# Token shift and turn of the gated part's features: from TensorE transposes to DRAM round trips and VectorE block transposes, in the middle blocks

## The chip, the cores and the metric

The kernel runs on one core of a Trainium2 chip. The metric is the device time of one execution in microseconds. The median of three runs of the kernel before is 3990.55 us (3989.72 to 3990.79). The profile is of one further execution with a time of its own.

## The reference

The input x is 8 sequences of 512 tokens with 256 features, fp32. A "macaron" of three parts runs over it: half of a local block, a global attention, half of a second local block (the same weights).

```python
x = x + 0.5 * ffn(layernorm(x));  x = x + attn(layernorm(x));  x = x + 0.5 * ffn(layernorm(x))

def layer(x):                                 # ffn: two layers of this, DEPTH = 2
    h = shift_token(x)                        # features 128..255 come from the token before (0 for token 0)
    q, k, v = split(h @ wqkv)                 # 8 heads of 64; l2norm, rotary, window of 128
    x = x + local_attention(q, k, v) @ wo
    h = shift_token(x)
    h = (h - mean(h)) / sqrt(var(h) + 1e-5) * lg + lb
    a, g = split(h @ w1 + b1)                 # the gated part, 682 hidden features
    return x + (a * gelu(g)) @ w2 + b2
```

The global attention has 16 heads of 16 features over all 512 tokens, each with its own 256x256 slice of the output weight. The change concerns the gated part from `h = shift_token(x)` to the input of `h @ w1`.

## The kernel before, in words

A sequence lies in SBUF as four tiles of 128 tokens (partitions) by 256 features, y[:, t, :]. Matrix products need the features on the partitions, so activations are turned again and again.

Three streams of work are recorded: streams 0 and 1 (`stream`), which each take four sequences through their first and second local block (eight blocks, n = 0 to 7, of two layers: `attention`, then `glu`), and the global stream (`global_heads`), which takes the sequences one by one through the 16 global heads between their two local blocks. All three are Python generators, pulled in turn; a `yield` ends a chunk. Nothing is issued at that time: `Plan.record` notes each operation with its rank (the order of recording) and its dependencies. `Plan.order` then writes out a fixed order for each engine: it runs through time with a cost for each operation (`Plan.cost`) and gives an engine, of the operations that can start within 40 ns of the first, the one of lowest rank. A tile is given a buffer of its tag's ring when its first user is placed. A DMA costs the plan 2000 ns, its bytes at 170 per ns behind the DMAs before it, and 300 ns; all of a DRAM tile counts as one region. `Plan.issue` emits the instructions in that order, so each engine and SP's queue work strictly in it, and on the chip semaphores hold each back until its data is there. Since one line issues everything, all rows of the profile bear L369 and are told apart by their tiles.

`FAR` marks the blocks whose attention turns by way of DRAM: n = 1 to 6. There the normed q and k are transposed by VectorE in blocks of 32 by 32 and `turned_far` writes the tile to DRAM and reads it back in four DMAs, one for each 32 partitions, so that the blocks come to their places; the attention weights go the same way (`turned_quarters`). In blocks 0 and 7, TensorE transposes against the identity (`transposed`).

The gated part (`glu`) has one form for all blocks. `shifted` turns the second half of the features with four TensorE transposes (operands const_ident, ypool_y), and VectorE copies the result out of PSUM one column to the right (zpool_z); column 0 is zeroed by GpSimd. Four more transposes turn it back (const_ident, zpool_z), and the PSUM bank `sh` holds the shifted half by tokens. VectorE takes statistics of both halves (`layernorm_stats`; GpSimd computes the power -1/2) and norms eight pieces of 128x128 into two tiles of tag qn (`normalize`). After the chunk's end, eight transposes turn these (const_ident, work_qn) into two PSUM banks, and VectorE scales them into hT, two tiles of tag z. Then come the products with w1 (zpool_z, wpool_w), gelu on ScalarE, the gate on VectorE, and the products with w2.

Tags have few buffers: z, qn and p have two for each stream, `both` two in all, and there are eight PSUM banks. All DMAs of the middle go through SP's queue.

Of the kernel before, what the change touches and what calls it, by code (L numbers as in the profile page):

```python
# [9 lines left out]
F32 = mybir.dt.float32  # L10
AF = mybir.ActivationFunctionType
ALU = mybir.AluOpType
# [3 lines left out]
P = 128  # L16
B, N, D = 8, 512, 256
NT = N // P
# [12 lines left out]
FAR = True  # L31
# [344 lines left out]
def macaron(ctx: ExitStack, tc: tile.TileContext, x, weight, wqkv, wo, w1, w2, b2, vecs, qk_scales, rotary, out):  # L376
    nc = plan = Plan()
# [4 lines left out]
    const, xpool, wpool, ypool, zpool, work = (pool(name) for name in ("const", "xpool", "wpool", "ypool", "zpool", "work"))  # L382
# [4 lines left out]
    xs = {}  # L387
# [40 lines left out]
    tabs, vec = [], []  # L428
# [46 lines left out]
    def layernorm_stats(halves, small=small):  # L475

        mv = small.tile([P, NT, 2], F32, tag="mv")
        for t, pieces in enumerate(halves):
            st = small.tile([P, len(pieces), 6], F32, tag="bnst", width=12)
            for i, piece in enumerate(pieces):  # L480
                nc.vector.bn_stats(st[:, i, :], piece)
            nc.vector.bn_aggr(mv[:, t, :], st.rearrange("p a b -> p (a b)"))
        ve = small.tile([P, NT], F32, tag="ve")
        nc.vector.tensor_scalar_add(ve, mv[:, :, 1], 1e-5)
        rstd = small.tile([P, NT], F32, tag="rstd")
        nc.gpsimd.tensor_tensor(rstd, ve, nhalf[:, :NT], ALU.pow)
        return mv, rstd

    def normalize(dst, src, mv, rstd, t):
        nc.vector.tensor_scalar(dst, src, mv[:, t, 0:1], rstd[:, t : t + 1], ALU.subtract, ALU.mult)  # L490
# [8 lines left out]
    def bank(shape):  # L499
        return psum.tile(shape, F32, tag="bank", width=N)  # L500

    def transposed(src, c):

        pt = bank([P, NT, P])
        for t in range(NT):
            nc.tensor.transpose(pt[:, t, :], src(t, c), ident)
        return pt.rearrange("p t q -> p (t q)")

    def shifted(src, k):

        z = zpool.tile([P, N + 1], F32, tag=f"z{k}", bufs=2)
        nc.gpsimd.memset(z[:, 0:1], 0.0)
        nc.vector.tensor_copy(z[:, 1:], transposed(src, 1))
        return z

    def turned_far(tile_):


        _, n, _, m, _ = tile_.shape
        flat = tile_.rearrange("p j b h c -> p (j b h c)")  # L520
        d = dram.tile([P, n, 4, m * 32], F32, tag="turned", bufs=8, width=2 * N)
        nc.sync.dma_start(out=d.rearrange("p j b m -> p (j b m)"), in_=flat)
        for b in range(4):
            rows = tile_[32 * b : 32 * b + 32].rearrange("q j a h c -> q j a (h c)")
            nc.sync.dma_start(out=rows, in_=d[:, :, b].rearrange("(a q) j m -> q j a m", a=4))
# [25 lines left out]
            rows = tile_[32 * b : 32 * b + 32].rearrange("q j a h c -> q j a (h c)")  # L551
            nc.sync.dma_start(out=rows, in_=d[:, :, :, b].rearrange("a q j m -> q j a m"))

    quarters_of = {}

    def attention(k, y, l, far):
        wqkv_sb, wo_sb = attention_weights[l]
# [248 lines left out]
            yield  # L806
        project(NT - 1, o)

    def glu(k, y, step, xb):
        l = step % DEPTH  # L810
        w1_sb, ends_sb, w2_sb = glu_weights[step]

        z = shifted(lambda t, c: y[:, t, c * P : (c + 1) * P], k)
        sh = bank([P, NT, P])
        for t in range(NT):
            nc.tensor.transpose(sh[:, t, :], z[:, t * P : (t + 1) * P], ident)
        hn = [work.tile([P, NT, P], F32, tag=f"qn{k}", bufs=2) for _ in range(2)]
        mv, rstd = layernorm_stats([[y[:, t, :P], sh[:, t, :]] for t in range(NT)])
        for t in range(NT):
            normalize(hn[0][:, t, :], y[:, t, :P], mv, rstd, t)  # L820
            normalize(hn[1][:, t, :], sh[:, t, :], mv, rstd, t)
        yield
        hT = []
        for c in range(2):
            h = zpool.tile([P, N + 1], F32, tag=f"z{k}", bufs=2)
            nc.vector.tensor_scalar(
                h[:, :N], transposed(lambda t, c: hn[c][:, t, :], c), vec[l][:, c : c + 1], vec[l][:, 2 + c : 3 + c], ALU.mult, ALU.add
            )
            hT.append(h)
        bias = vec[l][:, 4:].rearrange("p (s m) -> p s m", s=2)  # L830
        us = []
        for m in range(FULL):
            if m < 4:
                if m % 2 == 0:
                    pair = work.tile([P, 2, N], F32, tag=f"p{k}", bufs=2)
                u = pair[:, m % 2]
            else:
                u = work.tile([P, N], F32, tag=f"qn{k}", bufs=2)
            us.append(u)
            ag = {}  # L840
            for s in (1, 0):
                ag[s] = bank([P, N])
                with plan.together():
                    for c in range(2):
                        nc.tensor.matmul(
                            ag[s], lhsT=w1_sb[:, c, s, m * P : (m + 1) * P], rhs=hT[c][:, :N], start=(c == 0), stop=(c == 1)
                        )
            nc.scalar.activation(u, ag[1], AF.Gelu, bias=bias[:, 1, m : m + 1])
            nc.vector.scalar_tensor_tensor(u, ag[0], bias[:, 0, m : m + 1], u, ALU.add, ALU.mult)
            if m % 2 == 1:  # L850
                yield

        u = work.tile([P, N], F32, tag=f"qn{k}", bufs=2)
        us.append(u)
        nc.gpsimd.memset(u, 1.0)
        ag = bank([P, 2, N // 2])
        with plan.together():
            for turn in range(2):
                half = slice(turn * N // 2, (turn + 1) * N // 2)
                for c in range(2):  # L860
                    nc.tensor.matmul(
                        ag[: TAIL + LAST, turn],
                        lhsT=ends_sb[:, c, TAIL * turn : TAIL * turn + TAIL + LAST],
                        rhs=hT[c][:, half],
                        start=(c == 0),
                        stop=(c == 1),
                    )
        for turn in range(2):
            half = slice(turn * N // 2, (turn + 1) * N // 2)
            a_ = slice(TAIL * turn, TAIL * turn + LAST)  # L870
            g_ = slice(TAIL * (1 - turn), TAIL * (1 - turn) + LAST)
            nc.scalar.activation(u[a_, half], ag[g_, turn], AF.Gelu, bias=bias[g_, 1, FULL : FULL + 1])
            nc.vector.scalar_tensor_tensor(
                u[a_, half], ag[a_, turn], bias[a_, 0, FULL : FULL + 1], u[a_, half], ALU.add, ALU.mult
            )
        yield
        pys = {}
        for t in (0, 2, 1, 3):
            py = bank([P, D])
            pys[t] = py  # L880
            with plan.together():
                for m in range(FULL):
                    nc.tensor.matmul(py, lhsT=us[m][:, t * P : (t + 1) * P], rhs=w2_sb[:, m, :], start=(m == 0), stop=False)
            if t < 2:
                continue
            with plan.together():
                for at, q in ((0, t - 2), (TAIL, t)):
                    rows = slice(at, at + LAST + 1)
                    nc.tensor.matmul(
                        pys[q],  # L890
                        lhsT=us[FULL][rows, q * P : (q + 1) * P],
                        rhs=w2_sb[rows, FULL, :],
                        start=False,
                        stop=True,
                    )
            for q in (t - 2, t):
                nc.vector.tensor_add(y[:, q, :], pys[q], y[:, q, :])
                if l == DEPTH - 1:
                    nc.vector.scalar_tensor_tensor(xb[:, q, :], y[:, q, :], 0.5, xb[:, q, :], ALU.mult, ALU.add)
            yield  # L900

    def stream(k, blocks):

        for n, (b, second) in enumerate(blocks):
            while second and (b, True) not in done:
                next(others, None)
            y = layernorm(xs[b], k)
            yield
            for l in range(DEPTH):
                step = DEPTH * n + l  # L910
                yield from attention(k, y, l, FAR and 0 < n < len(blocks) - 1)
                yield from glu(k, y, step, xs[b])

                if k == 1 and step + 1 < DEPTH * len(blocks):
                    glu_weights.append(load_glu((step + 1) % DEPTH))
                if l == 0 and n + 1 < len(blocks) and blocks[n + 1][0] not in xs:
                    load_x(blocks[n + 1][0])
            done.add((b, False))
            if second:
                nc.sync.dma_start(out=out[b].rearrange("(t p) c -> p t c", p=P), in_=xs[b])  # L920
# [194 lines left out]
```

## Time and profile before

| what | value |
|---|---|
| median of three runs | 3990.55 us |
| the profiled execution's own time | 3989.82 us |
| its span | 3988.0 us |
| TensorE matmul, busy | 3924.2 us (98%), 24192 instructions |
| VectorE, busy | 2419.2 us (61%), 6832 |
| ScalarE, busy | 1780.9 us (45%), 4560 |
| GpSimd, busy | 1217.0 us (31%), 1154 |
| DMA, SP's queue | 357.00 MB, 381120 packets, 30.4% of 16 engines |
| granted TensorE clock, mean | 0.997 |

Engines: PE is TensorE's matmul, PEld its weight load (which lies beside matmuls), DVE is VectorE, ACT ScalarE, POOL GpSimd, SP SyncE, which only issues DMAs. Groups of instructions are shown as: line, engine, operation, what it writes <- what it reads, shapes, count | busy us in the union of its times, mean ns of one | idle time of the engine ahead of it and what ended that. Timelines are shown as start and length in us, then the merged instructions. A transpose on TensorE stands there as a matmul with const_ident. Ends of matmuls are modelled, so a busy TensorE is not one at its peak.

### The profile page before, as it was taken

The page shows a single profiled execution, that of the slowest core. Times are in us where ns is not written, and L with a number is a line of the kernel's source. Part 1 is how long each engine was busy: PE and PEld are TensorE (multiplying, and loading weights), DVE is VectorE, ACT ScalarE, POOL GpSimd, SP SyncE. Part 2 cuts the span into 40 slices and gives each one's busy share as a digit, 9 for nine tenths or more (in the row PEclk, how much of TensorE's full clock was granted, in tenths as well). Part 3 has the DMA queues.
Part 4 walks back from the last instruction along what each step waited for, and adds up shares of the span by engine and source line. Part 5 has one row for each costly group of instructions (what it writes and reads, how often), then busy time and mean ns, then how long its engine had stood idle before and what let it go on. Part 6 is the DMA issues. An engine that isn't in the chain of part 4 may idle for free.

```text
span 3988.0 us, 68204 instructions
## 1 busy us (share of the span) xinstructions
PE 3924.2 (98%) x24192; PEld 2714.1 (68%) x24192; DVE 2419.2 (61%) x6832; ACT 1780.9 (45%) x4560; POOL 1217.0 (31%) x1154
## 2 busy tenths in 40 slices
PE   8999999999999999999999999999999999999998
PEld 5565776767767667676666767767777667687665
DVE  7585655756556675665756657566547565535673
ACT  5564433534334454453444445344435343314562
POOL 6242413424224242332423324242214232103240
PEclk9999999999999999999999999999999999999999
DMA  3001533524335243352433524334225243210000
GB/s 115 3 21 35 151 92 110 150 82 119 92 117 147 76 123 100 103 150 73 145 96 108 149 73 127 93 120 132 82 70 149 72 126 95 65 32 9 1 23 11
DMA packets 382325, 362.69 MB, mean 91 GB/s; under 512 B 50880, under 2 KB 326944, under 8 KB 381984
## 3 DMA queue, kind: packets, MB, share of 16 engines
q1 hardware_dynamic: 381120, 357.00, 30.4%
q8 instruction: 192, 3.15, 0.3%
q10 hardware_dynamic: 864, 1.33, 0.1%
q14 instruction: 149, 1.22, 0.1%
HBM read 216.61 MB, written 124.78 MB: 86 GB/s over the span
## 4 chain that ended last, share of the span: by engine, by line
PE 83%; DVE 5%; ACT 2%; POOL 1%; issue 1%; DMA 0%; SPq 0%; DVEq 0%; ACTq 0%; POOLq 0%
PE psum_bank L369 83%; ACT work_p L369 2%; DVE work_qn L369 1%; DVE work_p L369 1%; DVE small_ss L369 0%; POOL small_rn L369 0%; DVE small_bnst L369 0%; DVE xpool_x L369 0%; POOL small_rstd L369 0%; DVE ypool_y L369 0%; DVE small_mv L369 0%; ACT work_qn L369 0%; POOL work_t L369 0%; ACT work_sq L369 0%; DVE work_both L369 0%
## 5 line engine op out<-in xcount | busy, mean ns | idle before, releaser
L369 PE MATMUL psum_bank<-work_xw,work_e 128*128 128x256 f32 x4096 | 957.1, 383 | 2.5 <-ACT work_e L369 1.4
L369 PEld LDWEIGHTS psum_bank<-work_xw,work_e 128*128 128x128 f32 x4096 | 760.5, 190 | 182.4 <-issue 39.2
L369 ACT ACTIVATE work_p<-work_p,small_nmax,small_rn 128x192 f32<-128x192 f32 (+2 forms) x1024 | 543.3, 532 | 369.9 <-DVE small_nmax L369 269.1
L369 PE MATMUL psum_bank<-wpool_wqkv,zpool_z 128*128 128x512 f32 x1536 | 702.6, 597 | 0.4 <-ACT zpool_z L369 0.3
L369 POOL TENSOR_TENSOR work_t<-work_qn,const_tab 128x256 f32<-128x256 f32 x512 | 382.7, 768 | 789.9 <-ACT work_qn L369 774.0
L369 PE MATMUL psum_bank<-zpool_z,wpool_w 128*128 128x512 f32 x1280 | 558.9, 595 | 1.3 <-DVE zpool_z L369 1.2
L369 POOL TENSOR_TENSOR work_p<-work_p,small_ri 128x768 f32<-128x768 f32 (+1 forms) x192 | 270.1, 1408 | 946.9 <-DVE small_ri L369 501.2
L369 POOL TENSOR_TENSOR small_rn<-small_ss,const_nhalf 128x8 f32<-128x8 f32 x256 | 480.5, 1878 | 107.3 <-DVE small_ss L369 100.9
L369 PE MATMUL psum_bank<-work_wa,work_gz 128*128 128x256 f32 x2048 | 479.7, 381 | 3.4 <-DVE work_gz L369 3.4
L369 PEld LDWEIGHTS psum_bank<-wpool_wqkv,zpool_z 128*128 128x128 f32 x1536 | 284.2, 191 | 279.4 <-issue 262.7
L369 ACT ACTIVATE work_e<-psum_bank 128x512 f32<-128x512 f32 x512 | 298.5, 596 | 356.2 <-PE psum_bank L369 355.9
L369 DVE SCALAR_TENSOR_TENSOR xpool_x<-psum_bank,gsmall_rinv,xpool_x 128x256 f32<-128x256 f32 x512 | 242.6, 475 | 335.6 <-PE psum_bank L369 332.3
L369 PEld LDWEIGHTS psum_bank<-zpool_z,wpool_w 128*128 128x128 f32 x1280 | 242.8, 191 | 296.8 <-issue 272.1
L369 PEld LDWEIGHTS psum_bank<-work_wa,work_gz 128*128 128x128 f32 x2048 | 383.0, 190 | 70.2 <-issue 11.0
L369 ACT COPY work_qn<-psum_bank 128x512 f32<-128x512 f32 x256 | 148.4, 582 | 422.7 <-PE psum_bank L369 351.0
L369 DVE TENSOR_REDUCE small_ss<-work_sq 128x8 f32<-128x512 f32 x256 | 173.4, 678 | 184.0 <-ACT work_sq L369 182.9
L369 PE MATMUL psum_bank<-wpool_wo,work_o 128*128 128x256 f32 x1024 | 245.8, 383 | 1.1 <-ACT work_o L369 0.7
L369 DVE SCALAR_TENSOR_TENSOR work_p<-psum_bank,const_vec,work_p 128x512 f32<-128x512 f32 x128 | 95.8, 749 | 243.6 <-PE psum_bank L369 146.4
L369 PE MATMUL psum_bank<-wpool_w,work_p 128*128 128x256 f32 x1024 | 243.1, 380 | 0.4 <-ACT work_e L369 0.4
L369 DVE COPY work_xw<-psum_bank 128x512 f32<-128x512 f32 x256 | 173.9, 680 | 114.0 <-PE psum_bank L369 112.6
L369 DVE CUSTOM_DVE_ANT_0 work_p<-psum_bank,const_near_mask 128x192 f32<-128x192 f32 x576 | 172.3, 352 | 93.6 <-PE psum_bank L369 91.4
L369 PEld LDWEIGHTS psum_bank<-wpool_wo,work_o 128*128 128x128 f32 x1024 | 190.2, 190 | 48.4 <-issue 16.1
(86 smaller groups left out, 4941.4 us busy)
## 6 DMA issues: line engine op xcount, KB each, us to landing
work_p<-dram_quarters SPq DMA_DIRECT2D x576, 128.0 KB
dram_quarters<-work_p SPq DMA_DIRECT2D x288, 192.0 KB
dram_turned<-work_both SPq DMA_DIRECT2D x96, 512.0 KB
work_both<-dram_turned SPq DMA_DIRECT2D x384, 128.0 KB
work_wa<-in_weight_dram SPq DMA_DIRECT2D x128, 256.0 KB
wpool_w<-in_w_dram SPq DMA_DIRECT2D x48, 640.0 KB
work_hT<-work_gz SPq DMA_DIRECT2D x512, 32.0 KB
dram_turned<-work_p SPq DMA_DIRECT2D x48, 256.0 KB
```

Source lines behind the costliest of these rows:

```text
L369: getattr(getattr(nc, op.engine), name)(*map(real, args), **{k: real(a) for k, a in kw.items()})
```

## The change

In the blocks n = 1 to 6 (`far`) the gated part gets its shifted half by way of DRAM: a DRAM tile for each stream, made once by `later`, holds 513 rows of 128 features with a row of zeros at its head. The second half of y is written to it from row 1 on, in two DMAs (tiles 0 to 2, then tile 3), and rows 0 to 511 are read back into an SBUF tile `sh` of tag qn. The normed features are written in an order by blocks of 32 columns into one tile of tag p; VectorE transposes this tile in place in blocks of 32 by 32, and `turned_far` places the blocks by one write to DRAM and four reads. hT is then scaled out of SBUF. Blocks 0 and 7 keep the form of before.

```diff
+    def later(k):
+        if k not in later_of:
+            zeros = work.tile([1, P], F32, tag="t2", bufs=2, width=N)
+            nc.gpsimd.memset(zeros, 0.0)
+            d = dram.tile([P, N + 1], F32, tag=f"later{k}")
+            nc.sync.dma_start(out=d[0:1, :P], in_=zeros)
+            later_of[k] = d.rearrange("p w -> (p w)").rearrange("(n f) -> n f", f=P)
+        return later_of[k]
...
-    def glu(k, y, step, xb):
+    def glu(k, y, step, xb, far):
...
-        z = shifted(lambda t, c: y[:, t, c * P : (c + 1) * P], k)
-        sh = bank([P, NT, P])
+        if far:
+            sh = work.tile([P, NT, P], F32, tag=f"qn{k}", bufs=2)
+            tokens = later(k)
+            for tiles in (slice(0, NT - 1), slice(NT - 1, NT)):
+                rows = tokens[1 + tiles.start * P : 1 + tiles.stop * P, :]
+                nc.sync.dma_start(out=rows.rearrange("(t p) f -> p t f", p=P), in_=y[:, tiles, P:])
+            nc.sync.dma_start(out=sh, in_=tokens[:N, :].rearrange("(t p) f -> p t f", p=P))
+        else:
+            z = shifted(lambda t, c: y[:, t, c * P : (c + 1) * P], k)
+            sh = bank([P, NT, P])
+            for t in range(NT):
+                nc.tensor.transpose(sh[:, t, :], z[:, t * P : (t + 1) * P], ident)
+        mv, rstd = layernorm_stats([[y[:, t, :P], sh[:, t, :]] for t in range(NT)])
+
+        if far:
+            hn = work.tile([P, 2, 4, NT, P // 4], F32, tag=f"p{k}", bufs=2, width=2 * N)
+            part = lambda c, t: hn[:, c, :, t, :]
+            split = lambda u: u.rearrange("p (b c) -> p b c", c=P // 4)
+        else:
+            hn = work.tile([P, 2, NT, P], F32, tag=f"p{k}", bufs=2, width=2 * N)
...
+            normalize(part(0, t), split(y[:, t, :P]), mv, rstd, t)
+            normalize(part(1, t), split(sh[:, t, :]), mv, rstd, t)
+        if far:
+            flat = hn.rearrange("p j b t c -> p (j b t c)")
+            nc.vector.transpose(flat, flat)
+            turned_far(hn)
         yield
...
+            if far:
+                to, back = to.rearrange("p (t a q) -> p t a q", t=NT, a=4), hn[:, c].rearrange("p a t q -> p t a q")
+            else:
+                back = transposed(lambda t, c: part(c, t), c)
+            nc.vector.tensor_scalar(to, back, vec[l][:, c : c + 1], vec[l][:, 2 + c : 3 + c], ALU.mult, ALU.add)
```

More of the change, by code (lines that the diff above doesn't have):

```diff
@@ L552, in turned_quarters @@
             nc.sync.dma_start(out=rows, in_=d[:, :, :, b].rearrange("a q j m -> q j a m"))
-    quarters_of = {}
+    quarters_of, later_of = {}, {}
+    def later(k):
[6 more added lines that the diff above has]
+        return later_of[k]
     def attention(k, y, l, far):
@@ L807, in attention @@
         project(NT - 1, o)
-    def glu(k, y, step, xb):
+    def glu(k, y, step, xb, far):
         l = step % DEPTH
         w1_sb, ends_sb, w2_sb = glu_weights[step]
-        z = shifted(lambda t, c: y[:, t, c * P : (c + 1) * P], k)
-        sh = bank([P, NT, P])
-        for t in range(NT):
[L816 to L821, printed above, removed]
+        if far:
[17 more added lines that the diff above has]
+            hn = work.tile([P, 2, NT, P], F32, tag=f"p{k}", bufs=2, width=2 * N)
+            part = lambda c, t: hn[:, c, t, :]
+            split = lambda u: u
+        for t in range(NT):
+            normalize(part(0, t), split(y[:, t, :P]), mv, rstd, t)
[4 more added lines that the diff above has]
+            turned_far(hn)
         yield
@@ L825, in glu @@
             h = zpool.tile([P, N + 1], F32, tag=f"z{k}", bufs=2)
-            nc.vector.tensor_scalar(
-                h[:, :N], transposed(lambda t, c: hn[c][:, t, :], c), vec[l][:, c : c + 1], vec[l][:, 2 + c : 3 + c], ALU.mult, ALU.add
-            )
+            to = h[:, :N]
+            if far:
[3 more added lines that the diff above has]
+            nc.vector.tensor_scalar(to, back, vec[l][:, c : c + 1], vec[l][:, 2 + c : 3 + c], ALU.mult, ALU.add)
             hT.append(h)
@@ L910, in stream @@
                 step = DEPTH * n + l
-                yield from attention(k, y, l, FAR and 0 < n < len(blocks) - 1)
-                yield from glu(k, y, step, xs[b])
+                far = FAR and 0 < n < len(blocks) - 1
+                yield from attention(k, y, l, far)
+                yield from glu(k, y, step, xs[b], far)
                 if k == 1 and step + 1 < DEPTH * len(blocks):
```

## The prediction

> **What bounds the kernel.** I read the page first (busy shares, the chain that ended last), then busy time by stretches, then the groups, then TensorE's timeline around one gated part.
>
> ```profile
> PE 3924.2 (98%) x24192; PEld 2714.1 (68%) x24192; DVE 2419.2 (61%) x6832; ACT 1780.9 (45%) x4560; POOL 1217.0 (31%) x1154
> ...
> PE 83%; DVE 5%; ACT 2%; POOL 1%; issue 1%; DMA 0%; SPq 0%; DVEq 0%; ACTq 0%; POOLq 0%
> ```
>
> ```profile
> 1180.00:1680.00 500.00, 497.25 (x3212) 343.88 (x3211) 309.28 (x875) 232.40 (x586) 160.51 (x150) 1.00 0.37 108
> 1680.00:2180.00 500.00, 496.01 (x3203) 341.12 (x3205) 318.39 (x887) 217.81 (x564) 171.06 (x159) 1.00 0.39 116
> ...
> 3580.00:3988.00 408.00, 384.92 (x2016) 257.18 (x2014) 233.80 (x658) 186.87 (x457) 104.16 (x97) 0.98 0.04 11
> ```
>
> The stretches' columns are length, then busy time of PE, PEld, DVE, ACT and POOL, clock, DMA share, GB/s. TensorE is busy 99.2% and 99.5% of the middle stretches at full clock, VectorE about 63%, the DMA engines under 40%. Only at the end, where no global work is left, does TensorE idle (23 of 408 us). So in the middle blocks TensorE's work is the price of the kernel, as long as it always finds something to do. The attention of the middle blocks already sends every turn through DRAM, and TensorE still has no holes there.
>
> **What goes.** Each gated part of a middle block loses 16 TensorE transposes: 4 that turn the second half of y, 4 that turn it back after the shift, 8 of the normed features. Six middle blocks, two layers, two streams: 24 parts, 384 transposes.
>
> ```profile
> L369 PE MATMUL psum_bank<-const_ident,work_qn 128*128 128x128 f32 x512 | 84.4, 285 | 16.6 <-DVE work_qn L369 16.0
> L369 PE MATMUL psum_bank<-const_ident,ypool_y 128*128 128x128 f32 x384 | 70.5, 288 | 17.0 <-DVE ypool_y L369 16.9
> L369 PE MATMUL psum_bank<-const_ident,zpool_z 128*128 128x128 f32 x128 | 19.3, 273 | 1.8 <-DVE small_ri L369 1.0 <-DVE zpool_z L369 0.8
> ```
>
> ```profile
> 1538.49 0.60 PE L369 MATMUL psum_bank<-const_ident,zpool_z 128*128 128x128 f32 x4
> 1538.93 3.62 PE L369 MATMUL psum_bank<-work_xw,work_e 128*128 128x256 f32 x16
> 1542.38 1.89 PE L369 MATMUL psum_bank<-work_wa,work_gz 128*128 128x256 f32 x8
> 1544.11 1.32 PE L369 MATMUL psum_bank<-const_ident,work_qn 128*128 128x128 f32 x7
> 1545.36 0.90 PE L369 MATMUL psum_bank<-work_p,work_v 64*64 64x128 f32 x32
> ```
>
> The mean of 273 to 288 ns holds the drain, which overlaps the next matmul, so it is no price. Start to start, the four zpool_z transposes take 0.44 us (1538.49 to 1538.93), 109 ns each: the floor, 384 x 0.109 = 41.9 us. The seven work_qn ones take 1.25 us (1544.11 to 1545.36), 179 ns each, since they keep pace with VectorE, which norms one tile after the other. Over all 24 parts of the trace, from each of these transposes' start to TensorE's next start, it is 134 ns for y, 116 for z, 163 for work_qn: 24 x (4 x 0.134 + 4 x 0.116 + 8 x 0.163) = 55.3 us. Busy time gives more, 24 x (4 x 0.184 + 4 x 0.151 + 8 x 0.165) = 63.8 us, drain included. Ends 42 and 55. The part above the floor is waiting, some of which comes back at other places, so I take 50.
>
> **VectorE.** Away: the copy of the turned half out of PSUM (0.687 us). Added: one block transpose of 128x1024. Rows: 694 to 701 ns for 512 elements, 964 for 768, so some 1.05 ns an element and 1.23 us. The two scalings that make hT read SBUF, not PSUM (802 ns now; 0.5 to 0.8). Four normings read SBUF, not PSUM (371 for 404 ns). Net -0.2 to +0.5 us a part, at most 12 us in 24 parts on an engine with 37% free: nothing on the path. Without that cover it would be those 12 us.
>
> The Trainium skill, "VectorE: DVE Perf Modes", section "Rules for kernel authors", speaks against this edit: a 128x128 transpose belongs on TensorE when PSUM may receive it, since VectorE turns blocks of 32 by 32 only; and "The three transpose paths" warns of turning by a DMA's strides (19 times slower than the crossbar). By the rule the work is on the right engine and the sum is 0 or worse. The rows: 128 columns cost VectorE 154 ns (1.23 / 8) and DMA time beside, TensorE 109 to 163. It is no cheaper work, but it moves from the engine that is 99% taken to one 63% taken. The trap does not bite, as after the block transpose each row moved holds 128 features in one run of 512 B; such packets are common in the trace (172,032, median 27 ns). The row decides.
>
> Second rule: "SBUF — State Buffer", terms and the engine side: VectorE in a two-port mode and GpSimd lock a shared port pair against each other for a whole instruction. 6 instructions a part become SBUF to SBUF. The trace's such norming: 308 least, 340 median, 1056 longest, mean 371. So the lock's price is some 31 ns: 144 x 0.031 = 4.5 us of VectorE. If each waited out the longest (0.7 us) it would be 101 us, still inside VectorE's slack of 1500, and hidden.
>
> **DMA and SP.** Per part: two writes of y's half (192 and 64 KB), a read of 256 KB, a write of 512 KB, four reads of 128 KB; all on SP. 8 x 24 = 192 issues, 0.35 to 0.6 us each by their like: 67 to 115 us on top of SP's 1293, hidden. 1.5 MB x 24 = 38 MB on 357, so the share goes from 30.4% to some 34%. Two waits are new on SP: the read of the shifted tile behind the 64 KB write, and the four reads behind the 512 KB write. Behind them stand the other stream's quarter reads, the copies into hT and the head's weights; engines that need those wait too. The order is planned by DMA costs that are longer than the chip's: the plan holds a 512 KB write for 5.4 us, the trace has 4.7 median (2.6 to 10.2) from such a write's issue to that of the read behind it. ACT and POOL do nothing new but 24 memsets fewer.
>
> **Latency of a stream.** From y's last tile to hT, the removed steps took some 3.2 us (0.6 y transpose, 2.05 copy and back, 0.5 turn). In their place: 64 KB write 3.6 (in SP's timeline the quarter writes of 1531.41 are followed by their reads at 1535.06), 256 KB read 2.4 (a lone weight load, issue to last packet), VectorE 1.2, then 4.7 + 4 issues 1.7 + last landing 2.4: 16.0. So +12.8 us a part, 12 parts a stream, 154 us. What hides it is the other stream and above all the global heads:
>
> ```profile
> 3562.57 3.62 PE L369 MATMUL psum_bank<-work_wa,work_gz 128*128 128x256 f32 x16
> 3566.12 1.14 PE L369 MATMUL psum_bank<-work_hT 16*128 16x512 f32 x8
> 3567.19 7.17 PE L369 MATMUL psum_bank<-work_xw,work_e 128*128 128x256 f32 x32
> 3574.20 3.62 PE L369 MATMUL psum_bank<-work_wa,work_gz 128*128 128x256 f32 x16
> ```
>
> From 3486 to 3601 TensorE runs heads alone, 11.63 us each, with no hole. So heads can fill any 13 us gap, and at the end of the middle blocks the streams stand 115 us ahead of them. Even if all 154 us were exposed, that lead and the 55 us saved cover it. I charge 5 us for new late landings (a fifth of a us a part; ends 0 and 45), because TensorE's own wait for DMA in this trace is 0.7 us over hundreds of turns.
>
> **Sum.** -50 + 5 = -45 us against the profiled execution's own 3989.82 (span 3988.0): 3944.8. The runs' median is 0.73 higher: 3945.5, so 3946.
>
> **Rivals.**
> A. The latency is exposed whole: streams end block 6 at 3484 + 154 = 3638, just where the last block starts now (3642), and the saved work turns to idle: 3987, no change. For it: ends of streams are chains of short steps. Against: 99% busy through the same kind of round trips in attention.
> B. Late landings hold in-order queues. VectorE's statistics wait for the shifted tile and its scaling for the turned one, so with each late landing all of VectorE stands, and TensorE after it. 48 landings; each late by 0.94 us eats the 45, by 1.1 us the kernel is slower. At 1.5 us late: 72 - 50 = +22, 4012. For it: GpSimd waited for quarter reads 77.6 us in 10 waits, ACT 29.3 for turned ones. Against: that is 20 waits in hundreds of landings, and the plan holds DMAs longer than they are.
> C. It does more than it says: four PSUM banks a part come free, and GpSimd's memset no longer waits for z (220.5 us of its waits in the whole kernel). TensorE's other stalls shrink by 10 us more: 3928.
>
> **How the numbers follow.** Likeliest case 0.66 (its own range 3934 to 3958), C 0.08, A 0.08, B 0.18. Range 3926 to 4004: it leaves the far part of B (0.13) and the far end of C. A difference under 0.2% (8 us) can't be told from none here. Faster 0.74, within 0.2% 0.08, slower 0.18.
>
> **What will show it.** TensorE 384 instructions fewer and some 45 us less busy; the middle stretches still at 99%; in TensorE's releasers no DMA of note; VectorE's busy time within 15 us of now; DMA share near 34%; the last block as long as now (346 us). Wrong if the middle stretches fall under 98.5%, VectorE shows waits on the read of the shifted tile, or the streams no longer finish ahead of the heads.

## The result, and the profile after

The changed kernel takes 3959.84 us (median of 6 runs, 3958.98 to 3962.59) against 3990.44 (3989.38 to 3990.79): 30.6 us less, ratio 0.9927 with a 95% interval of 0.9917 to 0.9938. The forecast was 3946, 45 us less; the measured time lies within the whole stated range (3926 to 4004) and just outside that of its likeliest case (3934 to 3958).

The page of the changed kernel, busy shares and the chain that ended last:

```profile
PE 3892.5 (98%) x23808; PEld 2675.0 (68%) x23808; DVE 2422.4 (61%) x6832; ACT 1779.5 (45%) x4556; POOL 1226.6 (31%) x1132
...
PE 55%; DVE 3%; ACT 2%; issue 2%; POOL 1%; DMA 0%; SPq 0%; POOLq 0%; DVEq 0%; ACTq 0%
```

TensorE has the 384 instructions fewer, but only 31.7 us less busy time. The chain's shares sum to some 63%, since it can be followed back to 1434.87 us only; the fall from 83% to 55% is that gap, and says nothing of TensorE.

Busy time by stretches of the changed kernel (columns as before):

```profile
1180.00:1680.00 500.00, 495.52 (x3260) 340.86 (x3259) 311.59 (x892) 218.84 (x569) 161.69 (x147) 0.99 0.42 123
1680.00:2180.00 500.00, 498.38 (x3078) 341.90 (x3077) 309.30 (x867) 220.88 (x581) 161.07 (x144) 1.00 0.42 124
...
3580.00:3958.00 378.00, 354.27 (x1875) 232.76 (x1873) 222.96 (x635) 179.66 (x433) 100.25 (x94) 0.98 0.03 9
```

The middle counts as full as before, 99.1% and 99.7%. But the column of the clock reads 0.99 in the first stretch, where the kernel before has 1.00. The mean granted clock is 0.994 to 0.996 in the six runs of the changed kernel, and 0.997 in the profile before; this comes back at the seam below. The groups of the changed kernel that answer to the removed and added work:

```profile
L369 PE MATMUL psum_bank<-const_ident,ypool_y 128*128 128x128 f32 x288 | 47.4, 289 | 16.8 <-DVE ypool_y L369 16.7
L369 PE MATMUL psum_bank<-const_ident,work_qn 128*128 128x128 f32 x256 | 38.4, 275 | 7.5 <-DVE work_qn L369 7.5
L369 DVE STREAM_TRANSPOSE work_p<-work_p 128x1024 f32<-128x1024 f32 x24 | 29.4, 1226 | 0.1
L369 DVE TENSOR_SCALAR zpool_z<-work_p,const_vec 128x512 f32<-128x512 f32 x48 | 26.4, 592 | 1.7 <-DMA work_p<-dram_turned 1.3 <-issue 0.2
```

The new work costs what was forecast, and VectorE waits for the placing DMA 1.3 us in all.

**Where TensorE's time went.** As in the prediction, TensorE's time was taken from each matmul's start to the next one's, and summed by what is read:

| read by TensorE | before, us | changed, us | |
|---|---|---|---|
| const_ident with work_qn and work_p (192 fewer) | 145.0 | 115.0 | -30.0 |
| const_ident with ypool_y (96 fewer) | 68.9 | 51.7 | -17.2 |
| const_ident with zpool_z (96 fewer) | 19.0 | 7.9 | -11.2 |
| the heads' work_xw, work_e | 908.0 | 918.9 | +10.8 |
| the heads' work_hT | 140.3 | 148.9 | +8.6 |
| all else | | | +8.8 |
| whole span | | | -30.2 |

(In blocks 0 and 7 the normed features now lie in a tile of tag p, hence the two names in the first row.) The transposes took 58 us with them, and 28 came back, 19 of it in two kinds of matmul of the global heads, whose instructions are the same ones as before. The experiments ask where these 28 us come from.

### The profile page after: what moved, and what is told of

It reads as the page before. It is cut to its first block, busy times and chain, and to the rows that moved or that the text cites. A ratio compares the mean times of both kernels' runs of the same rounds, so it can differ in the third digit from the quotient of the medians.

```text
span 3957.8 us, 67863 instructions
## 1 busy us (share of the span) xinstructions
PE 3892.5 (98%) x23808; PEld 2675.0 (68%) x23808; DVE 2422.4 (61%) x6832; ACT 1779.5 (45%) x4556; POOL 1226.6 (31%) x1132
## 3 DMA queue, kind: packets, MB, share of 16 engines
q1 hardware_dynamic: 436420, 394.76, 33.7%
## 4 chain that ended last, share of the span: by engine, by line
PE 55%; DVE 3%; ACT 2%; issue 2%; POOL 1%; DMA 0%; SPq 0%; POOLq 0%; DVEq 0%; ACTq 0%
PE psum_bank L369 55%; ACT work_p L369 1%; DVE work_p L369 1%; DVE work_qn L369 1%; POOL small_rn L369 0%; DVE small_ss L369 0%; POOL work_t L369 0%; SPq L369 0%; ACT work_qn L369 0%; DVE xpool_x L369 0%; DMA work_both<-dram_turned 0%; DMA work_p<-dram_turned 0%; ACT work_sq L369 0%; DVE work_both L369 0%; ACT work_both L369 0%
## 5 line engine op out<-in xcount | busy, mean ns | idle before, releaser
L369 DVE TENSOR_TENSOR ypool_y<-psum_bank,ypool_y 128x256 f32<-128x256 f32 x256 | 101.7, 419 | 216.2 <-PE psum_bank L369 213.2
L369 ACT COPY work_o<-psum_bank 128x512 f32<-128x512 f32 x128 | 74.7, 583 | 340.8 <-PE psum_bank L369 335.7
```

The source lines that it names most:

```text
L369: getattr(getattr(nc, op.engine), name)(*map(real, args), **{k: real(a) for k, a in kw.items()})
```

## The experiments

Three theories were set against each other. **Exposed latency**: the longer way from y to hT leaves TensorE without good work, and this lies in the written order. **Late landings**: DMAs land later than the order assumes, and in-order queues stand. **Chance of order**: any new order lies some 20 us off by luck. A fourth, TensorE's granted clock, was not among them; no run sets it apart, but every trace has it, and it is read beside the runs. Each run is compared with runs of the kernel before on the same chip.

**No round trips.**

```diff
-            sh = work.tile([P, NT, P], F32, tag=f"qn{k}", bufs=2)
...
-            nc.sync.dma_start(out=sh, in_=tokens[:N, :].rearrange("(t p) f -> p t f", p=P))
+            sh = y[:, :, P:]
...
             nc.vector.transpose(flat, flat)
-            turned_far(hn)
```

> Edit: the gated parts of blocks 1 to 6 lose the 384 TensorE transposes, but nothing goes by DRAM in their place: the second half is taken from y unshifted, and VectorE's 32x32 blocks are left where they are (the shift and the placing of the blocks are left out of the computation). The order of instructions is written anew for it. Theory (exposed latency: the removal is worth some 50 to 58 us of TensorE, and the longer way from y to hT gives 20 to 28 of it back): without the round trips the time falls by 48 to 56 us from the kernel before, to 3934 to 3943. Rival 1 (late landings: DMAs that come later than the order assumes hold in-order queues) expects the same here. Rival 2 (any new order costs about 20 us by chance, whatever is in it): 3950 to 3970, like the changed kernel.

Measured: 3940.32 against 3987.85, 47.5 us less (0.9882, 0.9867 to 0.9896). So the removal is worth 47.5 us, just under the 48 to 56 expected here; the forecast's gross gain of 50 nearly holds. (This kernel also needs one buffer of tag qn less in each part, which was not tested apart from the waits.) Summed as above, the transposes take 58 us away here too, work_hT falls by 3.3, and work_xw, work_e rises by 3.0. The whole change keeps 31 of the 47.5.

**The same order, its DMAs not issued.**

```diff
         for op in self.order():
+            if op.ghost:
+                continue
...
                 nc.sync.dma_start(out=rows.rearrange("(t p) f -> p t f", p=P), in_=y[:, tiles, P:])
+                plan.ops[-1].ghost = step > DEPTH
...
             turned_far(hn)
+            for op in plan.ops[-5:]:
+                op.ghost = True
```

> Edit: every engine's order is written as for the changed kernel, with all its DMAs, but in the gated parts of blocks 1 to 6 the write and four reads that place the blocks are then not issued, nor are the two writes of y's second half (save in each stream's first such part); the read of the shifted tile stays. The placing and the fresh shift are thus left out of the computation. Exposed latency: the loss lies in the written order, which spaces the work for these DMAs, so the time stays within 4 us of the changed kernel's 3959.8. Late landings: with no DMA to wait for, 15 to 25 us come back, 3935 to 3945. Chance of order: as exposed latency.

Measured: 3954.67 against 3987.85, 33.2 us less (0.9916, 0.9901 to 0.9931). The changed kernel's 30.6 and this lie within each other's intervals. Late landings were expected to bring back 15 to 25 us and brought some 3 (5 if the two kernels' medians are compared directly), so they are a small part of the 17 that are missing. The rest comes with the written order, which is the same in both. One hole can be seen in both. TensorE's timeline of the changed kernel, at the seam between the second and the third sequence of the global stream:

```profile
1244.66 0.85 PE L369 MATMUL psum_bank<-work_kT,work_qT 64*64 64x128 f32 x32
1245.44 1.13 PE L369 MATMUL psum_bank<-work_hT 16*128 16x512 f32 x4
1247.54 1.98 PE L369 MATMUL psum_bank<-work_hT 16*128 16x512 f32 x4 [0.97 <-DVE small_peak L369]
1250.02 3.30 PE L369 MATMUL psum_bank<-work_hT 16*128 16x512 f32 x8 [0.50 <-DVE work_xw L369]
1253.24 3.78 PE L369 MATMUL psum_bank<-work_xw,work_e 128*128 128x256 f32 x8
```

And of the kernel whose DMAs were not issued:

```profile
1245.86 1.13 PE L372 MATMUL psum_bank<-work_hT 16*128 16x512 f32 x4
1247.95 1.68 PE L372 MATMUL psum_bank<-work_hT 16*128 16x512 f32 x4 [0.97 <-DVE small_peak L372]
1250.43 3.29 PE L372 MATMUL psum_bank<-work_hT 16*128 16x512 f32 x8 [0.80 <-DVE work_xw L372]
1253.66 3.78 PE L372 MATMUL psum_bank<-work_xw,work_e 128*128 128x256 f32 x8
```

Sixteen matmuls on work_hT take 7.8 us (1245.44 to 1253.24), where a head's eight take 1.07 in the run of heads. These are the new sequence's first heads: they wait for VectorE, idle time of 0.97 and 0.50 us is named, and TensorE's order has nothing else to put in between. In the kernel before, this seam's first eight go at full pace, 1.07 us from this line's start to the next matmul's:

```profile
1255.52 1.14 PE L369 MATMUL psum_bank<-work_hT 16*128 16x512 f32 x8
```

The idle time is the smaller part of the hole. From 1249 to 1259 us the changed kernel's clock is at half (columns as in the stretches above; the clock is the third from the right):

```profile
1249.00:1259.00 10.00, 9.50 (x50) 5.96 (x50) 3.28 (x7) 7.16 (x25) 1.47 (x1) 0.50 0.67 198
```

So the eight matmuls on work_xw there take 3.71 us from start to start (1253.24 to 1256.95, where the next kind starts), 0.46 each, twice the 0.22 of the run of heads (7.01 us for 32). A matmul at half clock counts as busy for all of its doubled time. That is why the stretches stay above 99% while time is lost in them. The trace has two such stretches between 400 and 3580 us, 10.2 us here and 6.8 us at 3341, where the last sequence's first heads have just waited 0.82 us; the kernel before has none. The kernel whose DMAs were not issued has this one too (0.52 from 1249 to 1259 us).

What the clock is worth can be estimated: 0.001 of the mean clock is 0.001 x 3958 = 4 us, if TensorE had work throughout. The kernel with no round trips has a mean clock of 0.997, the changed one 0.995, so some 8 of the 17 us that are missing would be the clock. It is no noise between executions: the changed kernel's six runs have 0.994 to 0.996, 25 runs of the kernel before 0.996 to 0.998.

**A second round trip.**

```diff
             turned_far(hn)
+            turned_far(hn)
```

> Edit: the gated parts of blocks 1 to 6 make the round trip that places the blocks twice (write 512 KB, four reads, and again; the second one puts the blocks into wrong places, so features are mixed up from there on). Order written anew. Each part's way from y to hT gets some 8.8 us longer, 106 us per stream. Exposed latency: 20 to 28 us were lost for 154 us of added way; the next 106 cost more than in proportion, since the cover is used up first: 20 to 40 us over the changed kernel, 3980 to 4000. Late landings: one more pair of landings a part, 24 x 0.5 us, 3968 to 3975. Chance of order: 3950 to 3972.

Measured: 4004.1 against 3987.85, 16.2 us more (1.0042, 1.0027 to 1.0057), so 47 us more than the changed kernel, above the 20 to 40 set for it. (Its mean clock is 0.991; by the estimate above some 16 of the 47 would be the clock.) The stretches of this kernel:

```profile
1180.00:1680.00 500.00, 495.69 (x3154) 347.87 (x3153) 306.85 (x864) 210.34 (x575) 152.11 (x135) 1.00 0.44 132
...
3180.00:3680.00 500.00, 478.55 (x2968) 327.26 (x2970) 287.60 (x820) 205.37 (x545) 144.50 (x130) 0.98 0.36 108
```

The place shows: the global stream ends at 3540 us, while stream 1 starts its last block at 3655 only. In the kernel before the two stand at 3642 and 3645, in the changed one at 3612 and 3614. With the longer way the heads run ahead and are used up, and the streams' last middle blocks stand alone, with TensorE busy 478.6 of 500 us. The second trip also doubles the placing's DMAs, so it does not part latency from landings; the place does, since the heads have run out there.

**Half the change alone: the turn.** The shift's branch is taken as in the kernel before.

```diff
-        if far:
+        if False:
             sh = work.tile([P, NT, P], F32, tag=f"qn{k}", bufs=2)
```

> Edit: only the second half of the change: the shift stays on TensorE (8 transposes, VectorE's copy), the normed features are turned by VectorE and placed by DMA. 192 transposes fewer, worth 24 x 8 x 0.163 = 31 us by the trace. Its added way is 9.6 us a part, under two thirds of the whole. Exposed latency: cover is used up first by whichever comes first, so half the change gets more than half its gain: 22 to 28 us under the kernel before, 3962 to 3968. Late landings, or a loss in proportion: 12 to 18 us under, 3972 to 3978. Chance of order: anything from 3955 to 3985.

Measured: 3963.76 against 3987.85, 24.1 us less (0.9942, 0.9926 to 0.9959).

**The other half: the shift.** The branches of the turn are taken as in the kernel before.

```diff
-        if far:
+        if False:
             hn = work.tile([P, 2, 4, NT, P // 4], F32, tag=f"p{k}", bufs=2, width=2 * N)
...
-        if far:
+        if False:
             flat = hn.rearrange("p j b t c -> p (j b t c)")
```

> Edit: only the first half of the change: the shift goes by DRAM, the normed features are turned by TensorE as before. 192 transposes fewer, worth 24 x (4 x 0.134 + 4 x 0.116) = 24 us by the trace; the way from y to hT gets only 3.4 us longer a part (two short DMAs for 2.65 us of turning, copy and turning back). Exposed latency: so short an addition is nearly all covered, 18 to 24 us under the kernel before. Loss in proportion to transposes: 14 us under. Together with the turn alone (24 us under) the two halves then give more than the whole change, which had 31.

Measured: 3967.95 against 3988.64, 20.7 us less (0.9949, 0.9932 to 0.9965). The halves sum to 44.8, near the 47.5 of the removal; together they give 30.6. This fits a cover that hides two short additions and runs out under their sum. It is not shown: the gap is 14 us, the intervals are some 7 us each way, the mean clock is 0.996 to 0.998 in the halves' runs and 0.994 to 0.996 in the whole's, and an order alone moves as much (below).

**Chunk ends and a split read.**

```diff
-            nc.sync.dma_start(out=sh, in_=tokens[:N, :].rearrange("(t p) f -> p t f", p=P))
+                nc.sync.dma_start(out=sh[:, tiles], in_=tokens[tiles.start * P : tiles.stop * P, :].rearrange("(t p) f -> p t f", p=P))
...
+        if far:
+            yield
         mv, rstd = layernorm_stats([[y[:, t, :P], sh[:, t, :]] for t in range(NT)])
...
             turned_far(hn)
+            yield
         yield
```

> Edit: the whole change, its work and its DMAs kept, but recorded so that more of other streams' work ranks ahead of what waits for them: a chunk's end behind the shift's DMAs and a second one behind the placing's, and the shifted tile is read in two parts, tiles 0 to 2 as soon as their write is there (the plan sees the two parts as separate). Exposed latency: the 17 us between the changed kernel and the one with no round trips lie in the written order and come back in part: 6 to 15 us under the changed kernel, 37 to 46 under the kernel before. Late landings: at most 4 us under the changed kernel. Chance of order: anywhere within 10 us of the changed kernel.

Measured: 3941.36 against 3988.64, 47.3 us less (0.9877, 0.9863 to 0.9892): as much as with no round trips at all. Each part of it alone:

> Edit: the changed kernel with the two chunk ends alone; the shifted tile is read in one piece. Exposed latency: most of the 18 us that chunk ends and split read gave together comes from the ends, since they let other work rank ahead of the waiting chain: 8 to 15 us under the changed kernel. Chance of order: within 10 us of the changed kernel, either way.

Measured: 3940.92 against 3990.03, 49.1 us less (0.9878, 0.9863 to 0.9893).

> Edit: the changed kernel with the shifted tile read in two parts alone, no new chunk ends. Exposed latency: some 1 to 2 us of a part's way, 12 to 24 us a stream, at the rate of 0.11 to 0.4 us lost for each: 2 to 8 us under the changed kernel. Chance of order: within 10 us either way.

Measured: 3961.54 against 3990.03, 28.5 us less (0.9929, 0.9914 to 0.9944). The chunk ends do it all, more than the 8 to 15 us expected of them; the split read, of which 2 to 8 were expected, moves nothing that can be told. With chunk ends, the way from y to hT is not shorter: by the trace, from the end of y's last addition to hT's first scaling, 28.7 us median against 27.7. It is covered, with the same DMAs and no shorter wait. At this kernel's seam, TensorE's timeline shows the new sequence's first eight (1208.98) at full pace, with projections of a stream right behind them:

```profile
1207.17 1.88 PE L369 MATMUL psum_bank<-wpool_wqkv,zpool_z 128*128 128x512 f32 x4
1208.98 1.14 PE L369 MATMUL psum_bank<-work_hT 16*128 16x512 f32 x8
1210.05 5.42 PE L369 MATMUL psum_bank<-wpool_wqkv,zpool_z 128*128 128x512 f32 x12
1215.39 0.90 PE L369 MATMUL psum_bank<-work_p,work_v 64*64 64x128 f32 x32
1216.22 1.99 PE L369 MATMUL psum_bank<-work_xw,work_e 128*128 128x256 f32 x8
```

```profile
1205.00:1235.00 30.00, 30.00 (x247) 20.36 (x246) 25.49 (x77) 18.47 (x50) 17.77 (x15) 1.00 0.61 178
```

There is no wait here, and the clock is full here and through the whole middle. Its mean is 0.998, so by the estimate above some 12 of the 18 to 19 us that the chunk ends bring would be the clock. Whether the missing wait keeps the clock up is not shown by a run of its own; the two go together here.

**How far an order moves by itself.** The same instructions, with one constant of the plan changed, for both kernels.

```diff
-    SIGNAL = 110.0
+    SIGNAL = 115.0
```

> Edit: the changed kernel with one constant of the plan another, the delay it assumes for a signal between engines, 115 ns and not 110. Same instructions, another order. Exposed latency alone: within 5 us of the changed kernel, 30 us under the kernel before. Chance of order: 5 to 25 us away from it, since a greedy order shifts at a touch; then a part of the 17 us lost is no more than that.

Measured: 3985.47 against 3990.03, 4.6 us less (0.999, 0.9984 to 0.9997), which is 26 us above the changed kernel, where exposed latency alone allowed 5. The profile's mean clock is 0.993, so some 8 of the 26 would be the clock.

> Edit: the kernel before with the same constant at 115 ns. Both theories: within 10 us of the kernel before; how far it lies off, beside the run above, tells how much one order differs from the next when nothing else changes, and whether the change made the order more touchy.

Measured: 4004.27 against 3990.03, 14.2 us more (1.0035, 1.0023 to 1.0046). Both theories had allowed it 10. Its mean clock is 0.997 as before, so these 14 us are not the clock's. So 5 ns in the plan move the kernel before by 14 us and the changed one by 26, with no instruction added. At 115 ns the change is worth 18.8 us, at 110 ns 30.6. By start-to-start sums the 26 us are spread over many kinds of matmul, work_hT again first (+6.9).

**A larger offset between the streams.**

```diff
-LAG = 6
+LAG = 10
```

> Edit: the two chunk ends of the run above (the shifted tile read in one piece), and the first stream starts 10 chunks ahead of the second, not 6. Exposed latency: the two streams' gated parts come further apart from each other's waits; 48 to 60 us under the kernel before, more than either kernel gains. Chance of order: as the changed kernel, 20 to 40 under.

Measured, with the chunk ends: 3925.84 against 3988.64, 62.8 us less (0.984, 0.9825 to 0.9854). It is the fastest of all kernels here, and leaves nothing out.

> Edit: the kernel before, with the first stream 10 chunks ahead of the second, not 6; nothing else. Control for the run above. Exposed latency: the kernel before has waits in its attention too, so the offset alone is worth 5 to 15 us; the rest of the run above is the change's. Chance of order: 0 to 10 either way.

Measured: 3978.6 against 3988.64, 10.0 us less (0.9975, 0.9964 to 0.9985). Of the 62.8, 10 are the offset's without the change, though 10 us are less than an order moved by itself above.

## Why the prediction was right, point by point

- **The bound.** Right: TensorE's work is the price of the middle, and its removal alone brings 47.5 us. The reading of the 99% as "no holes" was too simple, since matmuls at half clock count as busy throughout; in the kernel before it did no harm, as its clock is full through the middle.
- **What goes.** Right: 50 us were taken between the ends 42 and 55, and the run without round trips measures 47.5. The transposes themselves left with 58 us, start to start.
- **VectorE.** Right: block transpose 1226 ns for 1.23 us, the scaling 592 ns mean within 0.5 to 0.8, the busy time 3.2 us higher. The rule of the transpose on TensorE would have given 0 or worse; the rows decided rightly. One reading is wrong and changes no number: after the block transpose, a run of 512 B in the placing's reads holds 128 tokens of one feature, not 128 features.
- **The port rule.** Its price was undersized, and hidden all the same: 4.5 us were put down, and the norming's mean rose to 405 ns from the 371 that this was taken from, as more of them now fall beside GpSimd (last section).
- **DMA and SP.** Right: SP's issues take 105.7 us more (67 to 115 forecast), the DMA share is 33.7% (34). VectorE waited 0.2 us in all for the shifted tile and 1.3 for the turned one.
- **Latency of a stream: the term that was mis-sized.** The way from y to hT rose from 10.3 us (median of 24) to 27.7, by 17.4 and not 12.8. The 64 KB write to its read is 1.75 us (3.6 taken) and the 512 KB write to its reads 3.9 (4.7); but from the read's issue to the first statistics 5.0 (2.4 taken), and from the end of the last of the four reads' issues to hT also 5.0 (2.4). As VectorE hardly waited for these landings, it is its other work, ahead in the written order, that stands between a landing and its user. "So heads can fill any 13 us gap" failed at the seam, where heads only start up. The charge of 5 us became 17 (47.5 less 30.6). It was charged to late landings, which are some 3 us of it by the run without those DMAs. For the clock the prediction put nothing; some 8 of the 17 go with it by the estimate above.
- **Rivals.** B, late landings, is refuted as the main loss in this kernel by that run. A, streams that end after the heads, does not occur (3612 and 3614 us), but a second round trip brings it about. C was not seen: other work on TensorE rose, and GpSimd's waits ahead of zpool_z went from 220.5 to 320.9 us. (C's own terms, 50 and 10, give some 3930 and not 3928.)
- **What would show it.** The last block is as long as before (344 us); TensorE's busy time fell by 31.7 us and not 45.

What stays open is how the 17 us divide. Late landings are a small part. For latency that is no longer covered stand the second round trip, which costs 47 us, more than any order here moved by itself, and the chunk ends: the three kernels with them gain 47.3, 49.1 and 62.8 us (52.8 beyond the offset's 10), the three whole changes without them 30.6, 28.5 and 4.6 (18.8 against the kernel before at the same 115 ns). Against it stands that a mere 5 ns in the plan moves 14 and 26 us, so one order more or less lucky could make the 17 too. A part goes with the clock, and no run tells whether waits bring the clock down or merely come with it. That the gain came out at 30.6 is in part luck of the order: at 115 ns it is 18.8. To tell these apart, many orders of each kernel would be wanted.

## What to carry to other kernels

Work taken off the bounding engine paid here nearly in full, 47.5 of 50 us, with no wait in its place, and as much in the kernels in which other work was ranked ahead of the wait. In the three kernels that have them, two words of recording order (`yield`) came with as much gain as no round trip at all, or more. Price an engine's relief by start-to-start times, and don't read 99% busy as full: look at the granted clock of the same stretch, since matmuls at half clock count as busy for twice the time. Where the order is written by a greedy plan, measure how far it moves at a touch before a gain of under 1% is put down to a change.

## What the runs showed of the hardware that was not expected

TensorE's granted clock fell to half for stretches of 3.4, 6.8 or 10.2 us between 400 and 3600 us in 11 of the 14 kernels here. Mostly they follow short waits: ahead of 24 of the 26 such stretches TensorE was idle for 0.4 to 3.3 of the last 3.4 us, ahead of two for 0.03 only. At the seam above, some 1 us of waiting was followed by 10.2 us at half clock.

VectorE's norming of 128x128 (now SBUF to SBUF in all middle blocks) takes longer beside GpSimd: 149 of them with no GpSimd instruction beside take 341 ns mean, 347 at most; 75 that overlap one take 531 mean, 330 to 1225. In the changed kernel's timeline:

```profile
2116.25 0.34 DVE L369 TENSOR_SCALAR work_p<-work_qn,small_mv,small_rstd 128x128 f32<-128x128 f32 x1
2116.34 1.52 POOL L369 TENSOR_TENSOR work_t<-work_qn,const_tab 128x256 f32<-128x256 f32 x2 [0.90 <-ACT work_qn L369]
2116.50 0.75 DVE L369 TENSOR_SCALAR work_p<-ypool_y,small_mv,small_rstd 128x128 f32<-128x128 f32 x1
2117.18 1.23 DVE L369 TENSOR_SCALAR work_p<-work_qn,small_mv,small_rstd 128x128 f32<-128x128 f32 x1
```

The norming that starts at 2116.50 takes 0.75 us beside GpSimd's products, the next 1.23, and the one that was under way when they started (2116.25) 0.34. The page "SBUF — State Buffer" of the Trainium skill, section "Who interferes with whom", describes an exclusive lock on a shared port pair, held for the whole instruction by whichever comes first, and these durations fit it. It costs (531 - 341) x 75 = 14 us of VectorE, hidden here. In the kernel before, 23 of 128 such normings overlap one (520 ns mean, 338 for the others), 4 us.
